# A transformer block on one core: the seams between attention and feed-forward rearranged, and another rule for single PSUM banks

## The chip, the cores and the metric

The kernel runs on one core of a Trainium2 chip. Its engines are TensorE (PE in the profile; PEld is its weight load), VectorE (DVE), ScalarE (ACT), GpSimd (POOL) and SyncE (SP). Each runs its own instruction stream strictly in order and waits for the others through semaphores. The metric is the device time of one launch in microseconds (us). A change of less than about 0.2% can't be told from none here.

## The reference

The input x has shape 8 x 1024 x 512 (batch, position, width), float32. A causal attention with 16 heads of 32 columns and a feed-forward of width 2048 each add a normalised result to x:

```python
def _layernorm(x, axis=-1, eps=1e-05):
    m = jnp.mean(x, axis=axis, keepdims=True)
    v = jnp.var(x, axis=axis, keepdims=True)
    return (x - m) / jnp.sqrt(v + eps)

# attention(h): q, v, k = split(h @ Wqvk); scores = q k^T, causal mask, / sqrt(512)
#               softmax over keys, times v, @ Wo
# ffn(x):       hidden = x @ W1 + b1
#               imag = w_imag * sin(theta + hidden * 0.1)
#               q = hidden + (cos(theta) * w_real + sin(theta) * w_imag) * imag * 0.1
#               relu(q) @ W2 + b2
x = x + _layernorm(attention(_layernorm(x)))
x = x + _layernorm(ffn(_layernorm(x)))
```

## The kernel before

The batches (`b`, 0 to 7) are worked through one after the other; a batch has eight tiles of 128 positions by 512 columns, in two halves of four tiles. All matrix products are float32.

**Attention of a batch** goes through four groups `g` of four heads. `find_maxima` (L434) computes the scores in four runs (`MAX_RUNS`), VectorE reads them from PSUM, adds the mask and takes each row's extreme value (L491, L503), ScalarE makes exponentials for the row sums of the first half (L523). Between the runs `advance(work, fill)` puts pieces of the next group's q, k and v projections (L374, L395) in TensorE's stream. Then ten units of key blocks follow, numbered `at` = 0 to 9: three for the first half of the queries, seven for the second (`KEY_UNITS`). In each, `weigh` computes transposed scores (L577, L588), ScalarE exponentiates them (L603, two instructions), GpSimd zeroes what the causal mask forbids in diagonal blocks (L607), and one unit later TensorE multiplies by v (L626). For the second half VectorE adds up the weights of all units in SBUF (L655, two instructions of 128x1024 in a full unit), TensorE sums them over the keys (L641), ScalarE and VectorE divide (`divide`, L657 to L663), which writes the last quarter of `wvT[1]`.

**Side work** is written as generators, one step at a time: `staged(n, *stages)` (L235) runs stage k on tile s-k in step s, last stage first. Attention advances one such generator, `more`, once per unit from unit number `first` on. In group 0 that is the end of the feed-forward of the batch before; in group 2 the first layer norm of the next batch (`norm1`); in group 3 `finish_block(b, 0, ...)`, from unit 4 on. What is left is done by `finish(more)` after the last sums.

**`finish_block`** (L751) takes four tiles of one half through five stages: `project` by Wo (L761, eight matmuls) with a ScalarE copy to SBUF (L770) and `measure`; `add` (normalise L230, add to x, L281); `measure` of x; `scale` (L230); `transpose` (four TensorE transposes L106, a ScalarE copy L248 into `x2T`). `measure` is bn_stats and bn_aggr on VectorE (`moments`, L215) and then, for the reciprocal deviation, two GpSimd instructions (`rstd_of`, L221: add eps, power -1/2). The first half's runs inside group 3 of the attention, the second half's inside the feed-forward (`between`).

**The feed-forward** (L785) has 32 steps of one 128-row block of hidden units for one half: `hidden(c)` (eight matmuls L806, ScalarE L814, VectorE L816 to L189, ScalarE's sine L821, VectorE L824 and L825) and, two steps later (`LAG`), `accumulate` (eight matmuls L833) into four PSUM banks `ys`. From step 2 on each step also advances `between`. `end(half)` (L842) adds b2 while it takes `ys` out of PSUM on VectorE (L847), and returns the stages measure, add, store. The end of the second half is handed to the next batch's attention as `rest`.

**PSUM** is one tile of eight banks, handed out at build time by `psum` (L81). `done_at` holds for each bank a count of when it was last emptied, or None while it is in use. A request for two banks takes the pair that has been empty the longest. A request for one bank prefers, before, a bank whose neighbour is in use, however lately the bank itself was emptied; the neighbour's pair is broken already.

Order: instructions marked `in_order` (or `keep_in_program_order`) keep the order of the program on their engine; the tile framework's scheduler places the others, at build time. Every engine's order is thus fixed before the run.

## Time and profile before

| what | us |
|---|---|
| median of three runs (3939.06 to 3939.67) | 3939.27 |
| the profiled execution, time of the launch | 3939.17 |
| its span, first to last instruction | 3937.4 |
| PE busy | 3810.8 (97%) |
| DVE busy | 2792.0 (71%) |
| ACT busy | 1504.8 (38%) |
| POOL busy | 545.7 (14%) |
| one batch, from attention's first score to the next batch's (batch 2) | 486.3 |

Times in the text below are of batch 2 unless said otherwise, in us from the start of the span. A line such as `1080.58 1.56 PE L641 ... [1.72 <-DVE w L655]` reads: from 1080.58 on, for 1.56 us, TensorE ran the instructions of line 641, after being idle for 1.72 us until VectorE's line 655 released it. In the list of waits, the numbers after the colon are us in total, how many times, and the longest. In the stages by window, each engine's busy time stands with its count of instructions in brackets, and the clock granted to TensorE (1.00 is full) before the last two numbers, the share and rate of the DMA.

### The profile page before, as it was taken

Reading aid. Unit: us, or ns where it says so; the run is one execution under the profiler, and the core shown is the slowest. Engines: PE = TensorE matmul, PEld = TensorE weight load, DVE = VectorE, ACT = ScalarE, POOL = GpSimd, SP = SyncE. Lnnn points to the kernel's source line nnn. Section 1 sums busy time; section 2 is a strip of 40 time slices with the busy share of each in tenths; the row PEclk is TensorE's granted clock in tenths of the full one; section 3 lists DMA queues with packets and bytes.
Section 4 is the critical chain, followed back from the end, with each engine's and each line's share of the span. In section 5 each row is a group of like instructions: output and inputs, shape, how many; then the busy total and the mean of one; then the engine's idle time right before and its main releaser. Section 6 shows DMA issues by size and latency. Waiting matters only on the chain.

```text
span 3937.4 us, 51398 instructions
## 1 busy us (share of the span) xinstructions
PE 3810.8 (97%) x19457; PEld 1759.9 (45%) x19457; DVE 2792.0 (71%) x6161; ACT 1504.8 (38%) x2804; POOL 545.7 (14%) x1131
## 2 busy tenths in 40 slices
PE   8999999999999999999999999999999999999998
PEld 4444444444444444444444444444444444444343
DVE  4777767777777777777777677766777766777666
ACT  4552145521465214642146421454214642155321
POOL 1220011200112001120012100111001120021200
PEclk9999999999999999999999999999999999999999
DMA  4000000000000001000000000000001000000000
GB/s 153 25 20 22 22 17 25 15 22 22 28 17 12 22 22 33 12 12 22 22 33 12 12 22 22 33 12 12 22 22 33 12 12 0 22 23 12 1 0 22
DMA packets 43496, 86.43 MB, mean 22 GB/s; under 512 B 4144, under 2 KB 4208, under 8 KB 42736
## 3 DMA queue, kind: packets, MB, share of 16 engines
q1 hardware_dynamic: 39056, 71.61, 5.6%
q10 hardware_dynamic: 4192, 11.53, 0.8%
q8 instruction: 152, 2.49, 0.3%
q14 instruction: 96, 0.79, 0.1%
HBM read 66.36 MB, written 16.78 MB: 21 GB/s over the span
## 4 chain that ended last, share of the span: by engine, by line
PE 85%; DVE 9%; ACT 2%; issue 2%; POOL 2%; DMA 0%; POOLq 0%; SPq 0%; DVEq 0%
PE banks L833 22%; PE banks L806 22%; PE banks L374 11%; PE banks L473 7%; PE banks L395 6%; PE banks L761 4%; PE banks L588 4%; PE banks L626 4%; DVE w L655 3%; PE banks L577 2%; DVE mx L491 2%; PE banks L106 2%; ACT w L603 1%; PE banks L641 1%; DVE st L218 1%
## 5 line engine op out<-in xcount | busy, mean ns | idle before, releaser
L806 PE MATMUL banks<-x2T,w_sb 128*128 128x512 f32 x2048 | 919.0, 593 | 5.4 <-ACT x2T L248 5.4
L833 PE MATMUL banks<-w_sb,hid 128*128 128x512 f32 x1536 | 691.3, 593 | 8.9 <-DVE hid L825 8.9
L603 ACT ACTIVATE w<-banks 128x1024 f32<-128x1024 f32 (+1 forms) x640 | 566.1, 937 | 284.4 <-PE banks L588 274.7
L806 PEld LDWEIGHTS banks<-x2T,w_sb 128*128 128x128 f32 x2048 | 386.0, 190 | 478.0 <-issue 468.8
L655 DVE TENSOR_TENSOR w<-w 128x1024 f32<-128x1024 f32 (+2 forms) x448 | 444.2, 1030 | 199.3 <-PE banks L626 168.3
L503 DVE CUSTOM_DVE_ANT_0 es<-banks,mask 128x128 f32<-128x128 f32 (+3 forms) x1024 | 432.6, 485 | 121.6 <-PE banks L473 121.6
L821 ACT ACTIVATE u<-u 128x512 f32<-128x512 f32 x256 | 161.1, 629 | 853.6 <-DVE u L189 853.5
L374 PE MATMUL banks<-xnT,wqvk_sb 128*128 128x512 f32 x1024 | 480.9, 609 | 3.0 <-DVE mx L491 3.0
L833 PEld LDWEIGHTS banks<-w_sb,hid 128*128 128x128 f32 x1536 | 291.2, 190 | 379.1 <-issue 335.1
L491 DVE TENSOR_REDUCE mx<-banks 128x1 f32<-128x512 f32 (+1 forms) x384 | 309.7, 861 | 116.9 <-PE banks L473 116.9
L607 POOL TENSOR_SCALAR_AFFINE_SELECT w<-w 128x256 f32<-128x256 f32 x512 | 292.6, 593 | 671.8 <-ACT w L603 664.1
L814 ACT ACTIVATE hid<-banks,prm 128x512 f32<-128x512 f32 x256 | 175.6, 686 | 502.2 <-PE banks L806 502.2
L626 PE MATMUL banks<-w,v 128*32 128x512 f32 (+3 forms) x3072 | 329.0, 496 | 22.8 <-POOL w L607 22.1
L588 PE MATMUL banks<-qk 32*128 32x512 f32 (+3 forms) x3072 | 327.9, 491 | 0.0
L816 DVE TENSOR_SCALAR u<-hid,prm 128x512 f32<-128x512 f32 x256 | 123.7, 483 | 282.5 <-ACT hid L814 282.1
L473 PE MATMUL banks<-qk 32*128 32x512 f32 (+3 forms) x3072 | 314.0, 513 | 0.3 <-DVE mx L503 0.2
L824 DVE SCALAR_TENSOR_TENSOR hid<-u,coef,hid 128x512 f32<-128x512 f32 x256 | 192.0, 750 | 162.7 <-ACT u L821 162.7
L374 PEld LDWEIGHTS banks<-xnT,wqvk_sb 128*128 128x128 f32 x1024 | 182.8, 190 | 243.3 <-issue 182.9
L523 ACT ACTIVATE es<-es,mx 128x512 f32<-128x512 f32 (+3 forms) x512 | 279.6, 550 | 2.0 <-DVE mx L503 2.0
L395 PEld LDWEIGHTS banks<-wqvk_sb,xnT 128*128 128x128 f32 x2048 | 239.0, 192 | 57.9 <-issue 34.4
L395 PE MATMUL banks<-wqvk_sb,xnT 128*128 128x128 f32 x2048 | 259.5, 280 | 0.0
L761 PE MATMUL banks<-wo_sb,wvT 128*128 128x512 f32 x512 | 233.5, 599 | 0.0
(96 smaller groups left out, 3371.2 us busy)
## 6 DMA issues: line engine op xcount, KB each, us to landing
xin<-in_L_attn_h_dram SPq DMA_DIRECT2D x112, 256.0 KB, 2.7
x<-in_L_attn_h_dram SPq DMA_DIRECT2D x64, 256.0 KB, 2.6
out_dram<-x SPq DMA_DIRECT2D x64, 256.0 KB, 2.0
w_tail<-in_L_ffn_W_dram SPq DMA_DIRECT2D x8, 1024.0 KB, 5.3
w_sb<-in_L_ffn_W_dram ACTq DMA_DIRECT2D x1, 4096.0 KB, 15.5
wqvk_sb<-in_L_attn_Wqvk_dram ACTq DMA_DIRECT2D x3, 1024.0 KB, 9.5
w_sb<-in_L_ffn_W_dram ACTq DMA_DIRECT2D x1, 3072.0 KB, 25.6
wo_sb<-in_L_attn_Wo_dram ACTq DMA_DIRECT2D x1, 1024.0 KB, 5.9
```

Of the source, the lines that this page charges most:

```text
L374: nc.tensor.matmul(pq, wqvk_sb[:, kc, c0 : c0 + P], xnT[b, half][:, kc, :], start=(kc == 0), stop=(kc == KC - 1),)
L395: nc.tensor.matmul(pv[:, t - t0, :], xnT[b, t // TPB][:, kc, (t % TPB) * P : (t % TPB + 1) * P], wqvk_sb[:, kc, c0 : c0 + P], start=(kc == 0),
L473: nc.tensor.matmul(scs[j // 2][:, j % 2, at : at + n], t[r, 0, i * P : (i + 1) * P], t[r, 1, k0 : k0 + n], start=True, stop=True,)
L491: nc.vector.tensor_reduce(out=mx[:, m], in_=sc[:, m, cols], op=ALU.min, axis=mybir.AxisListType.X,)
L503: nc.vector.tensor_tensor_reduce(out=es[:, m, cols], in0=sc[:, m, cols], in1=mask[:, HALF - n :], scale=1.0, scalar=FMAX, op0=ALU.add, op1 ...
L588: nc.tensor.matmul(sts[j // 2][:, j % 2, cols], t[r, 1, kb * P : (kb + 1) * P], t[r, 0, q0 : q0 + n], start=False, stop=True,)
L603: in_order(nc.scalar.activation(w[:, :, :width], st[:, :, :width], AF.Exp, scale=-1.0))
L626: nc.tensor.matmul(acc[r, HALF - n :], v[b, g][:, kb, r], weights[j // 2][:, j % 2, cols], start=first and k == 0, stop=last and k == len( ...
L655: in_order(nc.vector.tensor_add(t[:, :, q], t[:, :, q], w[:, :, cols]))
L761: nc.tensor.matmul(y, wvT[:, kc, t * P : (t + 1) * P], wo_sb[:, kc, :], start=(kc == 0), stop=(kc == KC - 1),)
L806: nc.tensor.matmul(ph, w1_sb[:, kc, fc * P : (fc + 1) * P], x2T[half][:, kc, :], start=(kc == 0), stop=(kc == KC - 1),)
L833: nc.tensor.matmul(ys[half, t], hids[c // 2][:, c % 2, t * P : (t + 1) * P], w2_sb[:, fc, :] if fc < NW2 else w2_tail[:, fc - NW2, :], sta ...
```

## The change

- `psum`: a request for one bank takes one with its neighbour in use only if at least two banks have been emptied since; otherwise the bank that has been empty longest.
- `finish_block` gets `by`, tiles per step, and its stages are written in itself. The first half (group 3) works on pairs, `by=2`: six steps instead of eight. Its reciprocal deviations come from ScalarE, `rstd_by_scalar`: Ln, then Exp of -1/2 of it, on 128x2 for a pair, instead of two GpSimd instructions for each tile. The second half keeps single tiles and GpSimd; its projection and measure are one stage as before.
- The second half's steps begin in step 0 of the feed-forward instead of step 2 (`if c <= LAG: advance(between)`).
- `end(1)` of every batch but the last: ScalarE copies `ys` out of PSUM and GpSimd adds b2; the sum into x is on GpSimd too. VectorE keeps the statistics and the normalising.
- In group 0, `find_maxima` advances that end once after each of its four runs, and the units take the rest.
- A constant tile `eps`; the buffers of some small tiles (3 instead of 4 for `st`).

Of the built program: ScalarE's stream gets 92 instructions (64 Ln and Exp, 28 copies), VectorE loses 56 (28 takings-out of PSUM, 28 additions), GpSimd loses 128 and gets 56 additions of 128x512 and one memset. TensorE and SyncE keep their counts.

```diff
@@ def psum
-        k = min(free, key=lambda k: (n == 1 and done_at[k ^ 1] is not None, max(done_at[k : k + n])))
+        def rank(k):
+            halved = n == 1 and done_at[k ^ 1] is None and done_at[k] + 2 <= clock[0]
+            return not halved, max(done_at[k : k + n])
+
+        k = min(free, key=rank)
@@
+    def rstd_by_scalar(mv, n):
+        rs = small.tile([P, n], F32, tag=f"rs{n}", name="rs", bufs=4 // n)
+        nc.scalar.activation(rs, mv[:, :, 1], AF.Ln, bias=eps)
+        nc.scalar.activation(rs, rs, AF.Exp, scale=-0.5)
+        return rs
@@ def find_maxima, after each of the four runs
             advance(work, fill)
+            advance(more)
@@ def attention
-            mT, later = find_maxima(b, g, work, sums)
+            more, first = after(g)
+            mT, later = find_maxima(b, g, work, sums, more if g == 0 else iter(()))
@@ def finish_block(b, half, wvT, x2T, by)
+        def tiles(n):
+            return range(n * by, (n + 1) * by)
+        def measure(n, source):
+            mvs[n] = small.tile([P, by, 2], F32, tag=f"mv{by}", name="mv", bufs=6 // by)
+            for t in tiles(n):
+                moments(source(t), mvs[n][:, t - n * by, :])
+            rss[n] = rstd_of(mvs[n], by) if half else rstd_by_scalar(mvs[n], by)
+        def project(n):
+            for t in tiles(n):
+                y = psum([P, D])
...
+                nc.scalar.copy(ys[t], y)
+                drained(y)
+            measure(n, lambda t: ys[t])
+        def add(n):
+            for t in tiles(n):
+                in_order(normalise(n, t, ys[t], ys[t]))
+                in_order(nc.vector.tensor_add(x(t), x(t), ys[t]))
+        def scale(n):
...
+        def transpose(n):
+            for t in tiles(n):
+                transpose_rows(xns[t], x2T[half][:, :, t * P : (t + 1) * P], nc.scalar.copy)
+        return staged(TPB // by, project, add, lambda n: measure(n, x), scale, transpose)
@@ def end(half)
+            spare = half and b + 1 < B
...
-                nc.vector.tensor_add(yb, ys[half, t], b2_sb)
+                if spare:
+                    in_order(nc.scalar.copy(yb, ys[half, t]))
+                    in_order(nc.gpsimd.tensor_tensor(yb, yb, b2_sb, ALU.add))
+                else:
+                    nc.vector.tensor_add(yb, ys[half, t], b2_sb)
...
+            def add(t):
+                in_order(normalised(ybs[t], ybs[t], mvs[t], rss[t]))
+                if spare:
+                    in_order(nc.gpsimd.tensor_tensor(x(t), x(t), ybs[t], ALU.add))
+                else:
+                    in_order(nc.vector.tensor_add(x(t), x(t), ybs[t]))
@@ feed_forward, step c
             if c < 2 * NFC:
                 hidden(c)
+            if c <= LAG:
+                advance(between)
             if c >= LAG:
                 accumulate(c - LAG)
             if c - LAG == NFC - 1:
                 rest = end(0)
-            elif c > 1:
+            elif c > LAG:
                 advance(between)
                 advance(rest)
@@ after(g)
-                return finish_block(b, 0, wvT[0], x2T), len(KEY_UNITS[0]) + 1
+                return finish_block(b, 0, wvT[0], x2T, 2), len(KEY_UNITS[0]) + 1
@@
-        rest = feed_forward(b, x2T, finish_block(b, 1, wvT[1], x2T))
+        rest = feed_forward(b, x2T, finish_block(b, 1, wvT[1], x2T, 1))
```

More of the change, by code (lines that the diff above doesn't have):

```diff
@@ L152 @@
     nc.gpsimd.memset(ones, 1.0)
+    eps = const.tile([P, 1], F32, tag="eps", name="eps")
+    nc.gpsimd.memset(eps, EPS)
     minus1 = const.tile([P, P], BF16, tag="minus1", name="minus1")
@@ L215, in moments @@
     def moments(src, mv):
-        st = small.tile([P, 6], F32, tag="st", name="st", bufs=4)
+        st = small.tile([P, 6], F32, tag="st", name="st", bufs=3)
         nc.vector.bn_stats(st, src)
@@ L223, in rstd_of @@
         if rs is None:
-            rs = small.tile([P, n], F32, tag=f"rs{n}", name="rs")
+            rs = small.tile([P, n], F32, tag=f"rs{n}", name="rs", bufs=4 // n)
         tc.keep_in_program_order(nc.gpsimd.tensor_scalar(rs, mv[:, :, 1], EPS, None, ALU.add))
         tc.keep_in_program_order(nc.gpsimd.tensor_tensor(rs, rs, mhalf[:, :n], ALU.pow))
+        return rs
+    def rstd_by_scalar(mv, n):
+        rs = small.tile([P, n], F32, tag=f"rs{n}", name="rs", bufs=4 // n)
+        nc.scalar.activation(rs, mv[:, :, 1], AF.Ln, bias=eps)
+        nc.scalar.activation(rs, rs, AF.Exp, scale=-0.5)
         return rs
@@ L249, in transpose_rows, with norm_stages @@
         drained(pt)
-    def norm_stages(source, own, dst, evacuate):
+    def norm_stages(source, dst, evacuate):
         mvs, rss, xns = {}, {}, {}
@@ L261, in scale @@
         def scale(t):
-            xns[t] = source(t) if own else tmp.tile([P, D], F32, tag="tmp", name="xn")
+            xns[t] = tmp.tile([P, D], F32, tag="tmp", name="xn")
             normalised(xns[t], source(t), mvs[t], rss[t])
@@ L268, in norm_stages @@
         return measure, scale, transpose
-    def residual_stages(target, y):
-        mvs, rss = {}, {}
-        def measure(t):
-            mvs[t] = one_mv()
-            moments(y(t), mvs[t][:, 0, :])
-            rss[t] = rstd_of(mvs[t], 1)
-        def add(t):
-            in_order(normalised(y(t), y(t), mvs[t], rss[t]))
-            in_order(nc.vector.tensor_add(target(t), target(t), y(t)))
-        return measure, add
     def advance(work, steps=1):
@@ L317, in norm1_first @@
         dst = new_xnT(0)
-        return staged(NT, *norm_stages(lambda t: xt[0, t], False, dst, nc.scalar.copy))
+        return staged(NT, *norm_stages(lambda t: xt[0, t], dst, nc.scalar.copy))
     moments_ahead = {}
@@ L432, with find_maxima @@
     )
-    def find_maxima(b, g, work, sums):
+    def find_maxima(b, g, work, sums, more):
         t = qk[b, g]
@@ L690, in attention @@
         for g in range(NG):
-            mT, later = find_maxima(b, g, work, sums)
+            more, first = after(g)
+            mT, later = find_maxima(b, g, work, sums, more if g == 0 else iter(()))
             mTs = [mT]
-            more, first = after(g)
             at = 0
@@ L749, in attention, with finish_block @@
             finish(more)
-    def finish_block(b, half, wvT, x2T):
+    def finish_block(b, half, wvT, x2T, by):
         x2T[half] = tp.tile([P, KC, HALF], F32, tag="t", name=f"x2T_{b}_{half}")
-        ys = {}
-        def project(t):
-            y = psum([P, D])
-            for kc in range(KC):
-                in_order(
-                    nc.tensor.matmul(
-                        y,
-                        wvT[:, kc, t * P : (t + 1) * P],
-                        wo_sb[:, kc, :],
-                        start=(kc == 0),
-                        stop=(kc == KC - 1),
-                    )
-                )
-            ys[t] = tmp.tile([P, D], F32, tag="tmp", name="yp")
-            nc.scalar.copy(ys[t], y)
-            drained(y)
+        ys, xns, mvs, rss = {}, {}, {}, {}
+        def tiles(n):
+            return range(n * by, (n + 1) * by)
@@ L773, in x @@
         def x(t):
             return xt[b, half * TPB + t]
-        measure, add = residual_stages(x, lambda t: ys[t])
-        return staged(
-            TPB,
-            lambda t: (project(t), measure(t)),
-            add,
-            *norm_stages(x, False, lambda t: x2T[half][:, :, t * P : (t + 1) * P], nc.scalar.copy),
-        )
+        def measure(n, source):
[3 more added lines that the diff above has]
+            rss[n] = rstd_of(mvs[n], by) if half else rstd_by_scalar(mvs[n], by)
@@ new lines, in normalise @@
+        def normalise(n, t, dst, src):
+            m = t - n * by
+            return normalised(dst, src, mvs[n][:, m : m + 1, :], rss[n][:, m : m + 1])
+        def project(n):
+            for t in tiles(n):
+                y = psum([P, D])
+                for kc in range(KC):
+                    in_order(
+                        nc.tensor.matmul(
+                            y,
+                            wvT[:, kc, t * P : (t + 1) * P],
+                            wo_sb[:, kc, :],
+                            start=(kc == 0),
+                            stop=(kc == KC - 1),
+                        )
+                    )
+                ys[t] = tmp.tile([P, D], F32, tag="tmp", name="yp")
+                nc.scalar.copy(ys[t], y)
+                drained(y)
+            measure(n, lambda t: ys[t])
@@ new lines, in add @@
+        def add(n):
[4 more added lines that the diff above has]
+            for t in tiles(n):
+                xns[t] = tmp.tile([P, D], F32, tag="tmp", name="xn")
+                normalise(n, t, xns[t], x(t))
+        def transpose(n):
+            for t in tiles(n):
+                transpose_rows(xns[t], x2T[half][:, :, t * P : (t + 1) * P], nc.scalar.copy)
@@ L846, in end, with x, measure @@
                 yb = tmp.tile([P, D], F32, tag="tmp", name="yb")
-                nc.vector.tensor_add(yb, ys[half, t], b2_sb)
+                if spare:
[3 more added lines that the diff above has]
+                    nc.vector.tensor_add(yb, ys[half, t], b2_sb)
                 drained(ys[half, t])
                 ybs.append(yb)
+            def x(t):
+                return xt[b, half * TPB + t]
+            mvs, rss = {}, {}
+            def measure(t):
+                mvs[t] = one_mv()
+                moments(ybs[t], mvs[t][:, 0, :])
+                rss[t] = rstd_of(mvs[t], 1)
+            def add(t):
[4 more added lines that the diff above has]
+                    in_order(nc.vector.tensor_add(x(t), x(t), ybs[t]))
             def store(t):
@@ L855, in store @@
                     load_x(b + 1, i)
-            return staged(
-                TPB,
-                *residual_stages(lambda t: xt[b, half * TPB + t], lambda t: ybs[t]),
-                store,
-            )
+            return staged(TPB, measure, add, store)
         rest = iter(())
```

## The prediction, made before the changed kernel had run

> **What bounds the kernel now.** I read the page first (who is busy), then the stages by window (where TensorE is not), then TensorE's waits in one batch (who ended its idle time), then the timelines at those places.

> ```profile
> PE 3810.8 (97%) x19457; PEld 1759.9 (45%) x19457; DVE 2792.0 (71%) x6161; ACT 1504.8 (38%) x2804; POOL 545.7 (14%) x1131
> ```

> TensorE is the bound; at most its 3937.4 - 3810.8 = 126.6 us of idle time can be won. Batch 2 by stage: group 0, 1, 2 and 3 of attention, each up to its L641, the rest of attention, the feed-forward; then group 0 of batch 0, which has no end of a batch before it to do:

> ```profile
> 1019.75:1080.58 60.83, 57.98 (x465) 27.86 (x465) 46.30 (x114) 31.94 (x64) 15.89 (x30) 1.00 0.11 34
> 1080.58:1135.91 55.33, 54.28 (x449) 25.93 (x449) 40.05 (x99) 32.56 (x65) 10.63 (x22) 1.00 0.07 23
> 1135.91:1196.13 60.22, 58.26 (x484) 28.67 (x480) 43.62 (x106) 36.91 (x73) 9.88 (x22) 1.00 0.07 19
> 1196.13:1266.92 70.79, 66.44 (x472) 30.65 (x469) 51.74 (x126) 35.88 (x71) 17.60 (x38) 1.00 0.05 16
> 1266.92:1269.25 2.33, 1.65 (x13) 0.58 (x13) 0.33 (x1) 1.17 (x3) 0.00 (x0) 1.00 0.04 11
> 1269.25:1506.05 236.80, 235.68 (x560) 104.76 (x560) 166.42 (x325) 49.20 (x75) 13.32 (x26) 1.00 0.06 18
> ...
> 44.48:102.83 58.35, 57.30 (x466) 27.70 (x465) 39.08 (x97) 33.59 (x66) 10.63 (x22) 1.00 0.00 1
> ```

> The feed-forward idles 1.12 us in 236.80, attention about 10.9. The clock is full throughout. In one batch TensorE waited for:

> ```profile
> PE banks L626 <- POOL w L607: 2.6, 4, 1.0
> PE banks L106 <- ACT v L403: 1.8, 4, 0.5
> PE banks L641 <- DVE w L655: 1.7, 1, 1.7
> PE banks L577 <- DVE mx L491: 1.4, 4, 0.4
> PE banks L577 <- ACT w L603: 1.2, 4, 0.5
> PE banks L833 <- DVE hid L825: 1.1, 1, 1.1
> PE banks L641 <- ACT x2T L248: 0.7, 1, 0.7
> PE banks L806 <- ACT x2T L248: 0.7, 1, 0.7
> ```

> The reader should sort them by what the change touches: the second and the two x2T waits are for a bank emptied a moment ago (bank rule); the third is group 0's overloaded VectorE; L833's is the start of the feed-forward; L626's is the seam after group 3, where the deviations on GpSimd stand before the mask.

> **The change part by part.** The sum is made against the profiled launch, 3939.17 us, 0.1 us below the median of the runs.

> *Bank rule.* In each group the transposes of the maxima (L106) take the bank that ScalarE is just emptying of v (L403): 4 x 0.46 = 1.8 us a batch; over the run the wait is listed as 14.3 us in 31. In the changed program's order that bank is one emptied 2.7 us of TensorE work earlier, and the v copy is no longer waited for. What is late next: the parts of the maxima are ready at 1054.65 (VectorE) and TensorE would come at 1055.47; GpSimd's masks for the following L626 end at 1055.08; so neither takes the wait over. Gain 14.3. The L577 waits for L491 keep their banks and stay; that for L603 in group 2 (0.5) gets a bank 0.7 us older: between 0 and 0.5 x 7, I take half, 1.8. The two x2T waits belong to the seam, below.

> *Group 0's end.* VectorE does four times normalise and add (L230 0.54 to 0.62, L281 0.69 to 0.77, together 5.2 us) between its weight additions, and TensorE waits at the sum:

> ```profile
> 1080.58 1.56 PE L641 MATMUL banks<-w,ones 128*32 128x512 f32 x8 [1.72 <-DVE w L655]
> 1135.91 1.07 PE L641 MATMUL banks<-w,ones 128*32 128x512 f32 x8
> ```

> After, the additions to x are GpSimd's, three of the four normalisings lie among the score runs and the fourth in the 5.12 us that VectorE idles before 1061.97. The same group without that work is batch 0's: 58.35 us against 60.83, and L641 itself 1.07 against 1.56: 2.48 + 0.49 = 2.97, times 7 batches, 20.8. What hides the moved work: VectorE idles 0.70, 0.39 and 2.46 us before the next score runs, each normalising takes 0.46 of pipe time, so the second sticks out by 0.07; the next reader of a bank comes later than that.

> *Taking ys out (seam into attention).* VectorE now has its four statistics in front of its first score run, and these wait for ScalarE's copy (0.59) and GpSimd's addition, which no row shows. Nearest below is a one-input mask of 256 columns, median 0.41, and of 128 columns, 0.295: 0.64 for 512. Nearest above is two-input power on 128x8, 1.83. I take twice the masks' mean of 0.593, 1.19, since the second input must be read too. The chain: first accumulation out at 1017.28, copy 0.59 and hand-over 0.07 give 1017.94; four additions 1022.70; the last statistics 0.69 and hand-over, 1023.42; the eight score instructions 2.82 and an aggregate 0.10, 1026.34. TensorE's next scores at 1026.24 take, by the changed order, exactly the banks that these read (before, one pair was long empty). So 0.1 x 7 = 0.7 lost; with 0.64 nothing, with 1.83 (4 x 0.64 more = 2.6 us later) 2.7 x 7 = 18.9. The same addition for x delays nobody: the masks of group 0 stand before the fourth, and the third is done some 2 us before the first mask.

> [...]

> *Start of the feed-forward.* The first L833 waits 1.12 us for its hidden block, which is ready 11.7 us after the first L806 starts. With three projections of 3.43 us put before it, L833 comes at 6 x 3.43 = 20.6 us. The projection itself now starts 3.43 us after L641's end instead of 10.3 and needs the quotient: 1268.08 to 1270.45 in the profile, 2.4 us after L641, so it is in time. VectorE's load in these first steps (4.3 us a hidden block, 3.6 a tile) stays below TensorE's 6.9 to 10.3 a step. Gain: the listed 8.9 us over eight batches.

> *Seam after group 3.* Here idle time is largest:

> ```profile
> 1260.29 0.84 PE L626 MATMUL banks<-w,v 128*32 128x384 f32 x4 [1.00 <-POOL w L607]
> 1261.64 1.06 PE L626 MATMUL banks<-w,v 128*32 128x384 f32 x12 [0.51 <-POOL w L607]
> ...
> 1258.99 0.22 POOL L225 TENSOR_SCALAR rs<-mv 128x1 f32<-128x1 f32 x1 [2.53 <-DVE mv L219]
> 1259.30 0.57 POOL L226 TENSOR_TENSOR rs<-rs,mhalf 128x1 f32<-128x1 f32 x1
> 1259.83 2.12 POOL L607 TENSOR_SCALAR_AFFINE_SELECT w<-w 128x256 f32<-128x256 f32 x4
> ```

> The power stands before the masks, TensorE idles 1.51 + 1.12 for masks and 2 x 0.68 for banks: 4.0 us a batch, 32 in all. Removing these is the upper bound. But VectorE is nearly full here (24 us of work between 1239.0 and 1266.8, 6 of idle), and its last weight addition releases L641. I walk the changed order with the rows' durations, from the same first projection at 1234.66. Projections in pairs end at 1241.8 and 1251.1. ScalarE's Ln and Exp (a 128x16 Ln takes 0.216) wait for the second tile of a pair: key 2's exponentials start at 1243.9 instead of 1242.95, VectorE idles 2.5, 1.5 and 1.3 us. From 1251.7 VectorE has no pause until the statistics of the last pair, 1260.75. Its Ln stands in ScalarE's queue before key 4's second exponential, which so ends at 1262.0; TensorE, there at 1258.6, waits about 3.4 us for it in L626. Masks then follow at once. VectorE's additions end at 1268.2 (before: 1266.8), L641 runs to 1269.3, and no transpose is behind it; L806 starts at 1269.3 where it was 1269.25. So I take 0.0: GpSimd's wait is replaced by ScalarE's, and VectorE ends last. Bounds: -4.0 x 8 = -32; and, if each of the three pair-waits costs another half microsecond, +1.5 x 8 = +12.

> Sum: -14.3 - 1.8 - 20.8 + 0.7 - 8.9 + 0.0 = -45.1. 3939.2 - 45.1 = 3894.

> **The rivals.**
> 1. *The seam pays too.* If VectorE gets through sooner without GpSimd's power beside it (L281 takes 0.77 instead of 0.69 then), the 32 us go as well: 3894 - 32 = 3862. Against: the walk has VectorE ending last. Chance 0.10.
> 2. *GpSimd's additions are late* at 1.83 us: 3894 - 0.7 + 18.9 = 3912. Chance 0.12.
> 3. *The bank wait only moves*: the shorter way to the maxima ends at the next L577, which waits for L491 or L603 in every group; then 14.3 + 1.8 are not won: 3910. Against: those waits hang on TensorE's own earlier matmuls and shift with them. Chance 0.09.
> 4. *Slower: ScalarE's queue at the seam.* Ln stands in front of exponentials and waits for VectorE, which waits for exponentials. If this loop costs 45.1 / 8 = 5.6 us a batch more than I walked, the change is worth nothing; from 6.7 us on (45.1 + 7.9, over 8) it is slower by over 0.2%; at 8 us, 3894 + 64 = 3958. For it: TensorE's 3.4 us wait in the walk. Against: the total of VectorE's work bounds it, and that hardly changes. Chance 0.07.

> **How the numbers follow.** My forecast, 3880 to 3908 about 3894, has 0.62. The range takes it and rivals 2 and 3 with a part of 1: 3870 to 3917; about 0.8. Faster by over 0.2% (below 3931) are the forecast and rivals 1 to 3, 0.93, less 0.02 for mixtures: 0.91. Rival 4 gives slower 0.06; same keeps 0.03. About 0.2%, 7.9 us, is what can be told from no change.

> **What would show each step.** Bank rule: no wait of L106 for L403, no L641 or L806 for L248. Group 0: 58.4 us from first score to L641, no wait for L655 there. Start: L833 after three projections without idle time. Ys: GpSimd's additions near 1.2 us, the second score run of group 0 without a wait. Seam: a wait of L626 for L603 of 3 to 4 us, L641 for L655, group 3 plus rest as long as before but for the bank wait (73.1 - 0.5). The prediction is wrong if group 3 grows by microseconds, or if VectorE's early statistics hold up the score runs.

## The result, and the profile after

The changed kernel takes 3897.88 us (median; 3897.77 to 3902.44) beside 3939.47 us for the kernel before: ratio 0.9897, 95% interval 0.988 to 0.9914. The forecast was 3894 with a range of 3870 to 3917. The profiled launch took 3897.95 us. Three of the four runs lie within 0.2 us at a mean granted clock of 0.994, the fourth took 3902.44 at 0.991.

Engines, on the page of the changed kernel, and then its stages by window in batch 2 (from, to and length; busy time of PE, PEld, DVE, ACT and POOL with counts of instructions in brackets; granted clock; DMA share and rate). The windows are the same six stages as before: groups 0 to 3 up to their L641, the rest of attention, the feed-forward.

```profile
PE 3802.8 (98%) x19457; PEld 1773.4 (46%) x19457; DVE 2759.4 (71%) x6105; ACT 1534.4 (39%) x2896; POOL 572.2 (15%) x1060
```

```profile
1011.11:1069.04 57.93, 57.35 (x466) 28.30 (x465) 43.62 (x109) 33.80 (x66) 21.81 (x37) 1.00 0.16 51
1069.04:1123.25 54.21, 53.63 (x452) 25.90 (x449) 39.68 (x98) 32.56 (x65) 10.58 (x22) 1.00 0.02 6
1123.25:1182.38 59.13, 57.71 (x484) 28.68 (x480) 43.39 (x106) 36.93 (x73) 10.03 (x22) 1.00 0.06 19
1182.38:1254.20 71.82, 66.89 (x476) 31.62 (x472) 51.69 (x126) 37.84 (x80) 11.97 (x22) 1.00 0.03 9
1254.20:1255.79 1.59, 1.59 (x11) 0.29 (x9) 0.55 (x1) 0.06 (x1) 0.00 (x0) 1.00 0.81 304
1255.79:1491.21 235.42, 235.42 (x563) 105.08 (x561) 164.89 (x322) 50.51 (x78) 17.56 (x28) 1.00 0.06 18
```

TensorE has no idle time left in the feed-forward (235.42 of 235.42), and every group of attention but the last is shorter. Its waits in that batch:

```profile
PE banks L626 <- POOL w L607: 3.3, 2, 2.4
PE banks L577 <- ACT w L603: 1.7, 4, 1.0
PE banks L577 <- DVE mx L490: 1.4, 4, 0.4
PE banks L111 <- DVE xin L244: 1.1, 2, 0.7
```

The waits for the v copy (L403 before, L402 now), for the `x2T` copies, for VectorE's weights at L641 and for the hidden block are gone. A wait for `xin` in the transposes of the next batch's first norm has grown from 4.1 to 7.7 us over the run. What is left in size is the seam after group 3. (Of the renumbered lines: 111 was 106, 244 was 230, 490 and 502 were 491 and 503, 778 was 761, 829 was 806, 856 was 833.)

Stage lengths in us; "expected" is taken from the prediction's terms.

| stage | before, batch 2 | after, batch 2 | difference | expected | over all batches |
|---|---|---|---|---|---|
| group 0 | 60.83 | 57.93 | -2.90 | -2.84 | -20.4 |
| group 1 | 55.33 | 54.21 | -1.12 | -0.95 | -8.2 |
| group 2 | 60.22 | 59.13 | -1.09 | -0.72 | -8.3 |
| group 3 and rest | 73.12 | 73.41 | +0.29 (to +1.6 in other batches) | -0.46 (the bank wait) | +6.8 |
| feed-forward | 236.80 | 235.42 | -1.38 | -1.12 | -11.1 |

The seam after group 3 in the changed kernel, in the timelines of TensorE, ScalarE, GpSimd and VectorE (start, duration, idle time before in brackets with its releaser):

```profile
1244.75 1.05 PE L626 MATMUL banks<-w,v 128*32 128x512 f32 x4 [0.89 <-POOL w L607]
1248.21 1.05 PE L626 MATMUL banks<-w,v 128*32 128x512 f32 x4 [2.40 <-POOL w L607]
...
1246.42 0.30 ACT L239 ACTIVATE rs<-mv,eps 128x2 f32<-128x2 f32 x1 [3.99 <-DVE mv L226]
1246.63 1.00 ACT L603 ACTIVATE w<-banks 128x1024 f32<-128x1024 f32 x1
...
1242.55 2.15 POOL L607 TENSOR_SCALAR_AFFINE_SELECT w<-w 128x256 f32<-128x256 f32 x1 [28.35 <-ACT w L603]
1247.75 0.41 POOL L607 TENSOR_SCALAR_AFFINE_SELECT w<-w 128x256 f32<-128x256 f32 x1 [3.05 <-ACT rs L240]
...
1250.03 4.72 DVE L655 TENSOR_TENSOR w<-w 128x768 f32<-128x768 f32 x6
...
1254.20 1.66 PE L641 MATMUL banks<-w,ones 128*32 128x512 f32 x8
```

The reader should see the loop that the prediction walked: ScalarE's Ln (L239) waits 3.99 us for the second mean of a pair, an exponential (L603) stands behind it, the mask (L607) behind that, and TensorE idles 0.89 + 2.40 = 3.3 us (3.4 was walked, under the name of L603). The first mask took 2.15 us where the second takes 0.41; that splits the wait in two, but its end is set by the second mask, which came after the late exponential. VectorE's additions end at 1254.75 and release the last four matmuls of L641, whose row takes 1.66 us for it.

One thing is new. Batch 2 above (counted from 0) runs at full clock; the same place in batch 3, cut into four windows of 3.41 us, doesn't:

```profile
1724.39:1727.80 3.41, 1.05 (x4) 0.14 (x4) 3.41 (x7) 0.99 (x2) 0.69 (x1) 1.00 0.00 0
1727.80:1731.21 3.41, 2.62 (x8) 0.95 (x9) 3.15 (x5) 2.13 (x4) 2.48 (x4) 0.50 0.00 0
1731.21:1734.62 3.41, 3.41 (x26) 1.74 (x28) 2.29 (x4) 2.15 (x4) 1.48 (x3) 0.50 0.00 0
1734.62:1738.03 3.41, 3.41 (x37) 1.73 (x30) 1.38 (x2) 1.55 (x4) 1.00 (x2) 1.00 0.88 292
```

TensorE was busy for 1.05 us in the first window and is then granted half its clock for two windows. Behind this seam that happens in six of the eight batches (an expectation below counts five; it leaves out the last). In the batches without it, 2 and 5, the seam (group 3 and rest) is 73.4 us long, with one slow window 73.8 to 74.0, with two 74.7; batch 7 is shorter as a whole and not compared. The kernel before has no such drop behind a seam.

### The profile page after: what moved, and what is told of

Same layout as the page of the kernel before. It is cut to its first block, busy times and chain, and to the rows that moved or that the text cites. A ratio compares the mean times of both kernels' runs of the same rounds, so it can differ in the third digit from the quotient of the medians.

```text
span 3896.2 us, 51378 instructions
## 1 busy us (share of the span) xinstructions
PE 3802.8 (98%) x19457; PEld 1773.4 (46%) x19457; DVE 2759.4 (71%) x6105; ACT 1534.4 (39%) x2896; POOL 572.2 (15%) x1060
## 4 chain that ended last, share of the span: by engine, by line
PE 92%; DVE 4%; ACT 2%; issue 2%; DMA 0%; POOL 0%; POOLq 0%; SPq 0%; ACTq 0%
PE banks L829 23%; PE banks L856 22%; PE banks L373 12%; PE banks L472 7%; PE banks L394 6%; PE banks L778 6%; PE banks L626 5%; PE banks L588 5%; PE banks L577 2%; PE banks L111 2%; DVE mx L490 2%; ACT w L603 1%; PE banks L641 1%; DVE st L225 1%; DVE w L655 1%
## 5 line engine op out<-in xcount | busy, mean ns | idle before, releaser
L829 PE MATMUL banks<-x2T,w_sb 128*128 128x512 f32 x2048 | 921.6, 593 | 0.0
L856 PE MATMUL banks<-w_sb,hid 128*128 128x512 f32 x1536 | 690.6, 593 | 0.0
L603 ACT ACTIVATE w<-banks 128x1024 f32<-128x1024 f32 (+1 forms) x640 | 566.6, 937 | 245.8 <-PE banks L588 240.5
L829 PEld LDWEIGHTS banks<-x2T,w_sb 128*128 128x128 f32 x2048 | 386.8, 190 | 476.5 <-issue 472.0
L655 DVE TENSOR_TENSOR w<-w 128x1024 f32<-128x1024 f32 (+2 forms) x448 | 448.0, 1034 | 213.2 <-PE banks L626 120.7
L502 DVE CUSTOM_DVE_ANT_0 es<-banks,mask 128x128 f32<-128x128 f32 (+3 forms) x1024 | 433.0, 486 | 125.7 <-PE banks L472 125.7
L373 PE MATMUL banks<-xnT,wqvk_sb 128*128 128x512 f32 x1024 | 480.9, 609 | 3.0 <-DVE mx L490 3.0
L856 PEld LDWEIGHTS banks<-w_sb,hid 128*128 128x128 f32 x1536 | 292.5, 190 | 366.7 <-issue 331.4
L607 POOL TENSOR_SCALAR_AFFINE_SELECT w<-w 128x256 f32<-128x256 f32 x512 | 297.1, 598 | 898.7 <-ACT w L603 863.2
L490 DVE TENSOR_REDUCE mx<-banks 128x1 f32<-128x512 f32 (+1 forms) x384 | 309.8, 862 | 103.9 <-PE banks L472 103.9
L626 PE MATMUL banks<-w,v 128*32 128x512 f32 (+3 forms) x3072 | 328.8, 500 | 27.4 <-POOL w L607 27.4
L472 PE MATMUL banks<-qk 32*128 32x512 f32 (+3 forms) x3072 | 315.3, 512 | 0.2 <-DVE mx L502 0.2
L373 PEld LDWEIGHTS banks<-xnT,wqvk_sb 128*128 128x128 f32 x1024 | 183.2, 190 | 243.0 <-issue 186.5
```

The lines of the kernel that those rows point to most:

```text
L373: nc.tensor.matmul(pq, wqvk_sb[:, kc, c0 : c0 + P], xnT[b, half][:, kc, :], start=(kc == 0), stop=(kc == KC - 1),)
L472: nc.tensor.matmul(scs[j // 2][:, j % 2, at : at + n], t[r, 0, i * P : (i + 1) * P], t[r, 1, k0 : k0 + n], start=True, stop=True,)
L490: nc.vector.tensor_reduce(out=mx[:, m], in_=sc[:, m, cols], op=ALU.min, axis=mybir.AxisListType.X,)
L502: nc.vector.tensor_tensor_reduce(out=es[:, m, cols], in0=sc[:, m, cols], in1=mask[:, HALF - n :], scale=1.0, scalar=FMAX, op0=ALU.add, op1 ...
L603: in_order(nc.scalar.activation(w[:, :, :width], st[:, :, :width], AF.Exp, scale=-1.0))
L626: nc.tensor.matmul(acc[r, HALF - n :], v[b, g][:, kb, r], weights[j // 2][:, j % 2, cols], start=first and k == 0, stop=last and k == len( ...
```

## The experiments

Differences are against the changed kernel's 3897.88 us; ratios are to the kernel before.

### The old choice of single banks

```diff
-            halved = n == 1 and done_at[k ^ 1] is None and done_at[k] + 2 <= clock[0]
-            return not halved, max(done_at[k : k + n])
+            return n == 1 and done_at[k ^ 1] is not None, max(done_at[k : k + n])
```

> The changed kernel with the old choice of single banks. Theory A (the rule takes away real waits for banks just emptied): a batch's groups 1 got 1.12 us shorter with the change, of which 0.49 was the late L641 of group 0, so 0.62 a group; 32 groups give 20 us, and group 0 of batch 0, which had no end to do, got the same 0.62 shorter (58.35 to 57.73). Time 3898 + 20 = 3918, and L106 waits for ScalarE's copy of v again, some 14 us in 31. Theory B (the waits only move to the next L577): 3898 to 3901.

Measured: 3957.34 us, ratio 1.0046 (1.0031 to 1.0061): 59.5 us above the changed kernel, and above the kernel before. Both theories missed it by far. From the waits of this kernel over the whole run (its lines have numbers lower by one):

```profile
PE banks L625 <- POOL w L606: 27.4, 18, 2.4
PE banks L576 <- ACT w L602: 18.3, 41, 1.1
...
PE banks L110 <- ACT v L401: 14.2, 31, 0.5
...
PE banks L777 <- ACT yp L786: 10.8, 16, 0.7
PE banks L110 <- ACT x2T L261: 10.8, 16, 0.7
```

The wait for v is back with its 14.2 us, as the bank theory has it. But there are two waits that neither kernel had: the second projection of each pair (L777) takes the bank that ScalarE is emptying of the first, and so do the paired transposes. Group 3 and rest takes 77.9 to 81.5 us in the first seven batches instead of 73.4 to 74.7; time at half clock, up to TensorE's last instruction, rises from 41.0 to 64.8 us. So the old rule is dear with pairs. Whether it is dear only with pairs is what the next run asked.

### The old choice of single banks, without pairs

```diff
-            halved = n == 1 and done_at[k ^ 1] is None and done_at[k] + 2 <= clock[0]
-            return not halved, max(done_at[k : k + n])
+            return n == 1 and done_at[k ^ 1] is not None, max(done_at[k : k + n])
@@ measure
-            rss[n] = rstd_of(mvs[n], by) if half else rstd_by_scalar(mvs[n], by)
+            rss[n] = rstd_of(mvs[n], by)
@@ after(g)
-                return finish_block(b, 0, wvT[0], x2T, 2), len(KEY_UNITS[0]) + 1
+                return finish_block(b, 0, wvT[0], x2T, 1), len(KEY_UNITS[0]) + 1
```

> The changed kernel with the old choice of single banks, and with the first half in single tiles with deviations by GpSimd, as before the change. The old choice alone had cost 59 us on the changed kernel. Theory A: most of that arises at the seam and only because pairs of tiles ask for two single banks at once; with single tiles the old choice costs what the group lengths of that run show, 0.7 us in group 0, 0.6 us in group 1 and 1.1 us in group 2, some 2.4 us a batch over 8 batches: 3884.9 + 19, so 3899 to 3906. Theory B: the old choice costs the same with single tiles, because single banks run short at the seam whoever asks: 3884.9 + 59, so 3940 to 3948.

Measured: 3911.23 us, ratio 0.9928 (0.9912 to 0.9945). It has to be held against the same kernel with the new rule, 3884.90 (below): the old rule costs 26.3 us with single tiles, 59.5 with pairs. That is theory A's side, 5 us above its range: in each of batches 1 to 6 the old rule lengthens group 0 by 0.40 to 0.70, group 1 by 0.62, group 2 by 1.09 and, left out of the expectation, the seam by 0.72 and the feed-forward by 0.36. In the seam stand again the two waits for `x2T` that the kernel before had too:

```profile
PE banks L110 <- ACT v L401: 1.8, 4, 0.5
...
PE banks L640 <- ACT x2T L261: 0.7, 1, 0.7
PE banks L828 <- ACT x2T L261: 0.7, 1, 0.7
```

These are waits of batch 2. With the new rule and single tiles one of the two x2T waits stays (L829, 5.4 us in eight). The rule and the pairs are thus one change in two parts: pairs can't be judged without the new rule.

### The second half taken up in step 2 again

```diff
-            if c <= LAG:
-                advance(between)
@@
-            elif c > LAG:
+            elif c > 1:
```

> The changed kernel, but the second half's projections begin in step 2 of the feed-forward again. Theory A: the first L833 waits 1.1 us for its hidden block again and the stage goes from 235.42 back to about 236.8 us, 8 x 1.39 = 11 us: 3909. Theory B (the seam before it had changed so that VectorE would be in time anyway): 3898.

Measured: 3909.05 us, ratio 0.9923 (0.9907 to 0.994), 11.2 us more. The wait of the first L856 for its hidden block is back, over the whole run:

```profile
PE banks L856 <- DVE hid L848: 8.9, 8, 1.1
```

From one batch's first feed-forward matmul to the sum of the next batch's group 0 it takes 294.75 us instead of 293.36, which is 1.39 a batch: the early start gives what the wait showed and 0.27 more.

### The end of the second half on VectorE, early and late

```diff
-            spare = half and b + 1 < B
+            spare = False
```

> The changed kernel, but VectorE takes ys out of PSUM and adds x, in the new early places. Theory A (what counts is that the work left the second-half units of group 0, whose VectorE is full; in the score runs there is idle time of 0.70, 0.39 and 2.46 us): the additions stick out by 0.3 to 1.1 us a batch: 3898 + 2 to 8 = 3900 to 3906. Theory B (what counts is that the additions left VectorE): all of the 3.0 us a batch comes back, 3898 + 21 = 3919.

Measured: 3902.57 us, ratio 0.9907 (0.989 to 0.9923), 4.7 us more. So theory A: with the early place kept, it matters little which engine adds. What it costs is seen at L373, which waits 9.4 us over the run for VectorE's maxima (L490) instead of 3.0.

Then the place alone, with the additions on GpSimd as in the changed kernel:

```diff
-            mT, later = find_maxima(b, g, work, sums, more if g == 0 else iter(()))
+            mT, later = find_maxima(b, g, work, sums, iter(()))
```

> The changed kernel, but the end of the batch before is not advanced between the score runs: statistics early as in both kernels, normalising among the second-half units, additions still on GpSimd. VectorE's extra work in those units is 4 x 0.54 = 2.2 us instead of 5.2. Theory A (VectorE's slack in these units is 5.2 - 3.0 = 2.2 us, so 2.2 us of work just fits): 0 to 0.5 us a batch, 3898 to 3902. Theory B (there is no slack, each microsecond of VectorE there costs one): 2.2 x 7 = 15, 3913.

Measured: 3959.85 us, ratio 1.0052 (1.0037 to 1.0067), 62.0 us more, four times theory B. From the timelines of this kernel in group 0 of batch 3:

```profile
1554.12 3.31 POOL L893 TENSOR_TENSOR x<-x,yb 128x512 f32<-128x512 f32 x1 [8.33 <-DVE yb L244]
...
1558.94 2.19 POOL L893 TENSOR_TENSOR x<-x,yb 128x512 f32<-128x512 f32 x1 [0.66 <-DVE yb L244]
...
1563.61 1.26 POOL L893 TENSOR_TENSOR x<-x,yb 128x512 f32<-128x512 f32 x1 [0.66 <-DVE yb L244]
...
1565.67 0.77 POOL L607 TENSOR_SCALAR_AFFINE_SELECT w<-w 128x256 f32<-128x256 f32 x2
...
1566.13 2.28 PE L626 MATMUL banks<-w,v 128*32 128x512 f32 x8 [4.79 <-POOL w L607]
```

GpSimd's queue holds three additions and the deviations between them ahead of the masks. Each addition waits for VectorE's normalise, each normalise for GpSimd's deviation, and the additions take 3.31 and 2.19 us beside VectorE's weight additions, against 1.26 alone. The mask starts 4.3 us after ScalarE's exponential ended at 1561.35, TensorE idles 4.79 us, and the clock is then halved for two windows from 1564.02. If this reading is right, the late place should be cheap again once the additions leave GpSimd. Both edits together:

> The changed kernel with the rest of the second half taken up where it stood before the change (behind the maxima of group 0), and its additions by VectorE as before the change. With the additions by GpSimd the late place had cost 62 us. Theory A: the late place costs so much because GpSimd's additions then stand ahead of the masks in GpSimd's queue; by VectorE it costs what group 0 lost before the change, 2.9 us in each of 7 batches, with some 5 us for the additions by VectorE: 3915 to 3926. Theory B: the late place costs it, whichever engine adds: 3950 to 3962.

Measured: 3917.25 us, ratio 0.9944 (0.9929 to 0.9959): theory A. Its list of waits over the run has the line of the kernel before back, and no mask that is late in group 0:

```profile
PE banks L626 <- POOL w L607: 27.4, 18, 2.4
...
PE banks L641 <- DVE w L655: 12.1, 7, 1.8
```

So the late place costs 14.7 us with VectorE (3917.25 - 3902.57) and 62.0 with GpSimd. GpSimd's help and the early place are again one change in two parts.

### A longer GpSimd addition

```diff
                     in_order(nc.gpsimd.tensor_tensor(yb, yb, b2_sb, ALU.add))
+                    in_order(nc.gpsimd.tensor_scalar(yb, yb, 0.0, None, ALU.add))
```

> The changed kernel with one more GpSimd instruction for each tile behind the addition of b2, an addition of 0.0 to the tile, which leaves the result as it is. The measured addition takes 1.27 us. Theory A (the chain of the prediction, from ScalarE's copy over four GpSimd additions to the fourth statistics and the eight score instructions, decides when the second score run of group 0 starts): four more instructions of about 0.64 us, 2.6 us later, nearly all on the path: 7 x 2.6 = 18 us, 3916, with L472 or its weight load waiting for L502 in group 0. Theory B (there is slack in it): below 3902.

Measured: 3966.66 us, the middle of two runs (3960.32 and 3973.01), ratio 1.0068 (1.0048 to 1.0088), 68.8 us more: in the direction of theory A and over three times its size. The extra pass (L875) takes 1.5 us a tile. VectorE's and TensorE's timelines in batch 3, from its run of 3960.32 us:

```profile
1512.98 0.70 DVE L225 BATCH_NORM_STATS2 st<-yb 128x6 f32<-128x512 f32 x1 [1.90 <-POOL yb L875]
...
1515.78 0.69 DVE L225 BATCH_NORM_STATS2 st<-yb 128x6 f32<-128x512 f32 x1 [1.82 <-POOL yb L875]
1516.39 0.27 DVE L502 CUSTOM_DVE_ANT_0 es<-banks,mask 128x128 f32<-128x128 f32 x1
...
1517.20 1.70 PE L472 MATMUL banks<-qk 32*128 32x512 f32 x2 [4.40 <-DVE mx L502]
```

The score instructions (L502), all but one of the first run's eight, stand behind the last statistics in VectorE's queue, and TensorE's next scores wait 4.40 us for the banks. The addition makes the fourth tile 4 x (1.49 + 0.09) = 6.3 us later, so the changed kernel had about 6.3 - 4.4 = 1.9 us of slack here. The prediction had put it at none (0.1 us short), since it let TensorE wait for all eight score instructions; here TensorE goes on at 1517.20, while the last of them are still to come (one starts at 1517.97). The rest is the clock:

```profile
1511.66:1515.07 3.41, 1.15 (x11) 0.95 (x9) 0.99 (x4) 0.87 (x3) 3.32 (x3) 1.00 0.00 0
1515.07:1518.48 3.41, 1.28 (x3) 0.97 (x4) 2.70 (x14) 1.77 (x7) 1.43 (x3) 0.50 0.00 0
1518.48:1521.90 3.42, 3.42 (x15) 2.35 (x12) 2.64 (x8) 1.98 (x9) 0.00 (x0) 0.50 0.02 5
1521.90:1525.31 3.41, 3.41 (x10) 1.44 (x8) 3.39 (x10) 0.00 (x0) 0.00 (x0) 1.00 0.00 0
```

Up to group 0's sum this kernel takes 7.4 to 7.7 us longer than the changed one in the batches where two windows are slow and 10.0 to 10.2 us where three are. Of that the wait is 4.4; the rest, 3.1 and some 5.7 us, is about half of the 6.8 and 10.2 us of slow windows.

### The seam: pairs or single tiles, ScalarE or GpSimd

Four corners, of which the changed kernel (pairs, ScalarE) is one. The edits are to the last argument of `finish_block(b, 0, ...)` and to the line of `rss[n]`, as in the diff further up.

Pairs with GpSimd's deviations:

> The changed kernel, pairs kept, but the first half's deviations on GpSimd again. In the changed kernel the seam (first projection to the first L829) takes 35.5 us where no clock drop falls in it, 34.6 before; TensorE idles 3.3 us in one place because Ln waits in ScalarE's queue before key 4's second exponential, and in five of eight batches the granted clock drops to 0.5 right behind it. Theory A (VectorE ends last there whatever computes the deviations; ScalarE's queue only shapes the idle time): seam 34.5 to 35.5 us without drops, 8 x 0 to 1 plus the five drops of about 0.3 to 1.3 us gone: 3885 to 3898. Theory B (ScalarE's blocked queue is itself the loss): the 3.3 us go, 8 x 3.3 = 26: 3872 or less.

Single tiles with ScalarE's:

> The changed kernel with single tiles in the first half, deviations still by ScalarE. Theory A (VectorE ends last): the singles let VectorE start earlier (it idles less than the 2.5, 1.8 and 1.0 us of the pairs), but the last two transposes stand behind the last units again: seam 33.5 to 35, 3882 to 3898. Theory B (Ln in ScalarE's queue is the loss, twice as many of them): slower than the changed kernel, 3900 to 3915.

Single tiles with GpSimd's, which is the seam as it was before the change:

> The changed kernel with the first half as before the change (single tiles, GpSimd), so that only the bank rule acts on the seam. Theory A (pairs and ScalarE do not pay): the seam is before's 73.1 us of group 3 and rest, less 0.6 for the maxima and 1.4 for the two x2T waits: 71.1 to 71.7, against 73.4 to 74.7 in the changed kernel, no clock drop there: 3898 - 8 x 2.3 = 3880, between 3875 and 3884. Theory B (pairs pay, because they keep GpSimd's power off the masks and the transposes ahead of the last units): 3900 to 3915.

| first half | us | ratio to before (95%) | seam, batch 2 | half clock |
|---|---|---|---|---|
| pairs, ScalarE (the change) | 3897.88 | 0.9897 (0.988 to 0.9914) | 73.41 | 41.0 |
| pairs, GpSimd | 3904.68 | 0.9911 (0.9896 to 0.9925) | 74.73 | 68.3 |
| single, ScalarE | 3883.67 | 0.9858 (0.9841 to 0.9874) | 72.24 | 20.5 |
| single, GpSimd | 3884.90 | 0.986 (0.9845 to 0.9875) | 72.41 | 10.2 |

"Seam" is group 3 and rest in us, "half clock" the time at half clock up to TensorE's last instruction (17.1 us in the kernel before). Pairs with GpSimd came out slower than both theories had it (3885 to 3898, and 3872 or less): the drops of the clock didn't go, they became more. Single tiles went the way of theory A in both runs (with GpSimd 0.9 us above its range): it is the pairs that cost, 14.2 us with ScalarE and 19.8 with GpSimd, and the choice of engine alone is worth 6.8 us in pairs and nothing that can be told in single tiles (1.2 us). With single tiles and ScalarE the loop is shorter: the Ln waits 2.50 us instead of 3.99 and TensorE's longest wait there is 1.76. Waits in this seam, single tiles with ScalarE:

```profile
PE banks L577 <- ACT w L603: 2.0, 2, 1.8
PE banks L829 <- ACT x2T L262: 0.7, 1, 0.7
```

The kernel with single tiles and ScalarE, the change without its pairs, has the lowest time of the study, 3883.67 us; its interval and the changed kernel's don't overlap, its interval and that of single tiles with GpSimd do.

### The deviations shared out

Since the one engine's stall is before L577 and the other's before L626, the last two runs gave each engine half of the deviations, with single tiles.

```diff
-        def measure(n, source):
+        def measure(n, source, own=False):
@@
-            rss[n] = rstd_of(mvs[n], by) if half else rstd_by_scalar(mvs[n], by)
+            rss[n] = rstd_of(mvs[n], by) if half or own else rstd_by_scalar(mvs[n], by)
@@ project
-            measure(n, lambda t: ys[t])
+            measure(n, lambda t: ys[t], True)
```

> Single tiles in the first half, the deviations of the projected rows by GpSimd and those of x by ScalarE. Theory A: the two queues share the waits, so each of the two stalls seen with one engine alone (1.8 us before the masked tiles' scores with ScalarE, 2.6 us before the masked tiles' products with GpSimd) falls by about half, some 1 us a batch: 3874 to 3880. Theory B: the stalls come from VectorE's moments, which are late behind its additions whoever takes the deviation: 3882 to 3888.

Measured: 3893.49 us, ratio 0.9884 (0.9869 to 0.9899). In the other mixture the condition is `half or not own`.

> Single tiles in the first half, the deviations of the projected rows by ScalarE and those of x by GpSimd. Theory A: as with the other mixture, 3874 to 3880. Theory B: 3882 to 3888; between the two mixtures, this one is the slower if the masks behind the deviation of x in GpSimd's queue are what TensorE waits for, by up to 1 us a batch.

Measured: 3888.81 us, ratio 0.9872 (0.9857 to 0.9886). Both theories fell (the second mixture is 0.8 us above theory B): sharing is slower than either engine alone, by 8.6 to 9.8 and by 3.9 to 5.1 us, and of the two mixtures the one named as the slower is the faster. In the first, timelines of VectorE, ScalarE and TensorE in batch 2:

```profile
1246.16 0.55 DVE L244 TENSOR_SCALAR yp<-yp,mv,rs 128x512 f32<-128x512 f32 x1 [0.86 <-POOL rs L233]
...
1245.33 0.29 ACT L239 ACTIVATE rs<-mv,eps 128x1 f32<-128x1 f32 x1 [3.29 <-DVE mv L226]
...
1246.82 0.28 PE L577 MATMUL banks<-mT,minus 32*128 32x256 bf16 x2 [2.35 <-ACT w L603]
1247.48 0.84 PE L626 MATMUL banks<-w,v 128*32 128x384 f32 x4
1248.65 1.87 PE L626 MATMUL banks<-w,v 128*32 128x384 f32 x12 [0.33 <-POOL w L607]
```

VectorE waits 0.86 us for GpSimd (0.51 for ScalarE when that takes all), so its later means come later, and ScalarE's Ln for x still holds the exponentials back: TensorE's longest wait is 2.35 us instead of 1.76. Which of these costs how much was not taken apart.

## Why the prediction was right or wrong

Total: 45.1 us were predicted and 41.6 measured. No term failed in kind, but four were mis-sized, and that the total is so near is in part luck: by stage, groups 1 and 2 and the feed-forward gave some 6 us more than was put, and the seam took 10 more.

**Bank rule.** Sized at 14.3 + 1.8 = 16.1 us in the groups; the runs with single tiles show 26.3 for the rule: 17.5 in groups 0 to 2, 5.7 at the seam and 2.9 in the feed-forward. "I take half" for group 2's wait for L603 was too low: the wait is gone whole (0.52), and group 2 gained 1.09 where 0.46 + 0.26 had been put. It gained that although its wait for `xin` grew from 0.58 to 1.07, because TensorE's busy time there fell too (58.26 to 57.71). Group 1 gained 0.62 from the rule against a listed wait of 0.46; the other 0.16 is busy time as well. Why TensorE is busy for less isn't settled. What the prediction didn't see is that pairs need the new rule: under pairs the old one costs 59.5 us instead of 26.3. Rival 3, that the wait only moves, is out: L577's waits for L490 are 11.0 us before and after, and putting the old rule back lengthens the groups.

**Group 0's end.** Predicted 2.48 + 0.49 = 2.97 a batch, 20.8. Putting the work back (late, on VectorE) costs 3917.25 - 3897.88 = 19.4. Group 0 needs 57.93 us, the predicted 58.4 less the bank wait, and L641 has no wait. That its cover lies in VectorE's pauses between the score runs was right.

**Taking ys out.** Predicted 0.7 with a GpSimd addition of 1.19 us, between bounds of 0.64 and 1.83. On the changed kernel's list of groups (busy us, mean ns; idle before):

```profile
L893 POOL TENSOR_TENSOR x<-x,yb 128x512 f32<-128x512 f32 x28 | 35.5, 1267 | 115.0 <-DVE yb L244 115.0
L874 POOL TENSOR_TENSOR yb<-yb,b_sb 128x512 f32<-128x512 f32 x28 | 34.6, 1267 | 640.3 <-ACT yb L873 640.3
```

It is 1.27 us, a little above the 1.19 taken, and still nothing is lost: the second score run starts without a wait, with about 1.9 us to spare. At the bound of 1.83 the fourth addition would come 4 x 0.56 = 2.2 us later, just past that slack; so rival 2's condition would, as an estimate from the run with the longer addition, have cost some tenths of a microsecond a batch, not 2.7.

**Start of the feed-forward.** Predicted 8.9 us, the listed wait; taking it back costs 11.2. L856 comes after three projections and without idle time, as the prediction has it.

**Seam after group 3.** Here the size was furthest off: "so I take 0.0". Group 3 and rest grew by 6.8 us over the run although seven bank waits of 0.46 had left it, so the term itself measures about +10, near the upper of the bounds of -32 and +12. The walk itself held: a wait of 3.3 us at L626 behind ScalarE's Ln, where 3.4 was walked, and VectorE ending last (it had even less room than was read: 4.3 us of idle time between 1239.0 and 1266.8, not 6). Batches that keep the full clock are 0.29 us longer than before, 2.3 us over eight; the other 4.5 come from windows at half clock behind the 3.3 us of idle time, which a walk with durations from rows at full clock can't hold. Group 3 growing by microseconds was the prediction's own sign of being wrong; the worst batch grew by 1.6. The ground for the 0.0, that VectorE ends last whatever GpSimd is relieved of, holds for pairs alone: with single tiles and ScalarE the seam is 0.9 us shorter than before and 1.2 shorter than with pairs.

Rival 1, that the seam pays too, is out with pairs. Its ground isn't in the profile of before either: there L281 took 0.69 us beside GpSimd's power (at 1247.78) and 0.77 beside masks (at 1260.55). Rival 4, ScalarE's queue at the seam, is the mechanism that took place, at about a fifth of the price from which it would have decided (1.25 us a batch above the walk against 6.7). Waits of another kind did reach such a price in two variants: with the old bank rule under pairs, or with GpSimd's additions ahead of the masks, the same change was slower than the kernel before.

## What to carry to other kernels

Before helping a full engine by a second one, read what already stands in the second one's queue: GpSimd's additions were free ahead of group 0's masks and cost 62 us among them. Parts that look separate can hang together (pairs and the bank rule, GpSimd and the early place), so undo them one by one and in twos, and drop the one that doesn't pay: here the pairs, for 14 us. And count a wait of TensorE as a risk of half clock behind it: in the traces here, from 150 us on, it followed every 3.41 us window at full clock that waits had left busy for less than 0.47. That cost 0.3 to 1.3 us a batch at the seam with pairs, 3 to 6 us in group 0 with the longer addition, and nothing at the seam with single tiles and ScalarE.

## What the runs showed of the hardware that was not expected

```profile
1239.90:1243.31 3.41, 1.65 (x20) 0.83 (x16) 2.87 (x8) 2.36 (x6) 0.61 (x1) 1.00 0.00 0
1243.31:1246.72 3.41, 3.28 (x23) 1.55 (x20) 3.27 (x6) 2.03 (x6) 3.06 (x6) 0.50 0.56 184
```

TensorE is busy for 1.65 us of 3.41, 0.48, in the first window. There the drop cost nothing: the seam takes 72.2 us in each of the first seven batches, with a drop or without. This is read from windows that came about by themselves; a run that only fills the idle time wasn't made. The drop at 3.58 to 3.65 ms, once in every run, follows windows that the records call busy for 0.84 or more; it lies in the last batch's last group, where scores have no projections among them (42 matmuls in 9.78 us before, against 24 in 2.0 elsewhere). Whether TensorE is really idle inside those records is open.

**GpSimd's additions beside VectorE's.** The 128x512 addition L893 takes 1.26 us alone (at 1563.61 in the kernel with the late place and GpSimd's additions) and 3.31 and 2.19 beside L655 (at 1554.12 and 1558.94); a mask instruction, of which the median is 0.41 in the changed kernel, took 2.15 at its seam (at 1242.55, beside L655). Why they take longer there no run shows.
